# A TensorE multiply for every gathered row block in layer 3 of a graph network

## The chip, the core and the metric

The kernel runs on one NeuronCore of a Trainium2 chip. The metric is the time on the device in microseconds (us), the median of several executions. One execution is also profiled; its trace gives the start of each instruction on TensorE (PE, with its weight loads as PEld), VectorE (DVE), ScalarE (ACT), GpSimd (POOL) and SyncE (SP), the packets of the DMA engines, and the clock that TensorE was granted.

## What is computed

A graph of 3125 nodes (256 features each) and 50000 edges goes through four layers. Each layer is a graph step and a feed-forward step (mixture of experts or selected tokens), each added to the node features. The change touches the graph step of the last layer, which takes for every node the maximum over its neighbours' projected features:

```python
x = x + _L3_gnn_ref(_layernorm(x, axis=-1), edge_index, ...)

def _L3_gnn_ref(x, edge_index, W_proj, b_proj, W_l, b_l, W_r, gamma, beta):
    n = x.shape[0]
    loops = jnp.arange(n, dtype=edge_index.dtype)
    src = jnp.concatenate([edge_index[0], loops])
    dst = jnp.concatenate([edge_index[1], loops])
    xp = jax.nn.relu(x @ W_proj.T + b_proj)
    agg = jax.ops.segment_max(xp[src], dst, num_segments=n)
    out = agg @ W_l.T + b_l + x @ W_r.T
    out = jax.nn.relu(out)
    mean, var = jnp.mean(out, axis=0), jnp.var(out, axis=0)
    return (out - mean) * jax.lax.rsqrt(var + BN_EPS) * gamma + beta
```

## The kernel before

The nodes are ordered by their number of incoming edges and cut into NT = 25 tiles of 128, one node per partition. A tile's edges are processed in rounds: in one round every node of the tile takes one neighbour. RND lists the rounds of each tile (32 for the first, 9 for the last), OFF their running sum, and SR = 413 is their total. The few edges beyond these rounds go through a loop (`rounds_beyond`, `body3`) that runs only when there are any.

The program is one stream of instructions for each engine. The layers before this stage use a planner that orders the instructions by estimated costs. Layer 3's graph step doesn't use it: its loop stands in a `manual_schedule` block, so each engine gets its instructions in the order in which the code is written.

At the end of layer 2 the projected features relu(x W_proj + b) are written to the DRAM table `tab3`, and kept in ACC, where they are the node's own contribution to the maximum. XN holds the normalized features. Then the stage runs as follows.

- `look(r)` (L2376) takes a buffer of 128x256 from a pool of ROWS = 24 buffers and has GpSimd gather one row of `tab3` into each partition (an indirect DMA; the instruction is recorded under the helper's line L136). Round r's gather is issued right after round r - 24 has been used, and 24 are issued ahead of the loop.
- For each tile, TensorE transposes the tile's features XN (`turned`, L1651, two transposes into a PSUM bank of the tag `tp`), and ScalarE copies them to g_xt (L1653).
- For each round of the tile, VectorE takes the maximum of ACC and the gathered block (L2395), in place.
- At the seventh round of a tile, VectorE takes the batch statistics of the tile before it (`stats`, L2384), which read that tile's result Y (c_y in the profile).
- After the tile's last round, TensorE transposes the maxima (L1651), ScalarE copies them to g_at (L1653), and TensorE multiplies in two halves of 128 output features: two products with W_r on g_xt (L2405) and two with W_l on g_at (L2407), added up in one bank of the tag `mm`. ScalarE applies bias and relu and writes Y (L2408).

The PSUM banks of the stage are set by the call `psums(tp=3, mm=4)`: three for transposes, four for products. The matrices are float32. The identity used in transposes is `ident`. After the stage the statistics are combined (L2414) and the feed-forward step of layer 3 follows (from L2422), again under the planner, with expert products (L1982, L1986), gathers of expert results (ro_g) and the scatter of the output.

The shared helper `turned` and the gathering helper:

```python
    def gather(dst, table, idx):
        return nc.gpsimd.indirect_dma_start(
            out=dst, out_offset=None, in_=table, in_offset=bass.IndirectOffsetOnAxis(ap=idx, axis=0))
```

Of the kernel before, what the change touches and what calls it, by code (L numbers as in the profile page):

```python
# [13 lines left out]
OP = mybir.AluOpType  # L14
# [5 lines left out]
P = 128  # L20
# [75 lines left out]
def tile_gnn_ffn(ctx: ExitStack, tc: tile.TileContext, a: dict, out: bass.AP):  # L96
    nc = tc.nc
# [6 lines left out]
    @contextmanager  # L104
    def psums(**bufs):
        with tc.tile_pool(name="psum", bufs=1, space=PSUM) as p:
            before = dict(banks)
            banks["pool"], banks["bufs"] = p, bufs
            yield
            banks.update(before)  # L110

    def ps(tag, shape):
        return banks["pool"].tile(shape, F32, name=tag, tag=tag, bufs=banks["bufs"][tag])
# [35 lines left out]
    ident = per.tile([P, P], F32, name="ident")  # L149
# [96 lines left out]
    def load_w(pool, w, name):  # L246

        k, n = w.shape
        t = pool.tile([P, k // P, n], F32, name=name)
        nc.sync.dma_start(t, w.rearrange("(k p) n -> p k n", p=P))  # L250
        return t
# [207 lines left out]
    with tc.If(uns > 0):  # L459

        rec = dram.tile([E, RW], F32, name="rec")
        with tc.tile_pool(name="srt", bufs=1) as ep, tc.tile_pool(name="srt2", bufs=2) as eb, \
# [25 lines left out]
            for b in range(ET // BT):  # L488
                s = slice(b * BT, (b + 1) * BT)
                n = BT * EP  # L490
                row = eb.tile([P, n], I32, name="s_row")
# [24 lines left out]
                r = eb.tile([EP, BT, RW], F32, name="s_rec")  # L516
# [10 lines left out]
            for b in range(ET // BT):  # L527
                s = slice(b * BT, (b + 1) * BT)
                r = eb.tile([EP, BT, 8], F32, name="s_back")
# [932 lines left out]
    with tc.tile_pool(name="f1", bufs=1) as fp, tc.tile_pool(name="f1b", bufs=2) as fb, psums(mm=3, y=3, tp=2):  # L1462
# [60 lines left out]
        with tc.If(tie > 0):  # L1523

            with tc.tile_pool(name="f1t", bufs=1) as tp_:
                row = tp_.tile([P, NX], F32, name="f_row")
# [50 lines left out]
        for t in range(NT):  # L1577
            nc.tensor.matmul(pl.rearrange("p i k -> p (i k)"), fl[:, t, :], vals[:, t].rearrange("p i k -> p (i k)"),
                             start=(t == 0), stop=(t == NT - 1))
# [264 lines left out]
    class Experts:  # L1844
# [292 lines left out]
        def combine(self, t):  # L2137
# [7 lines left out]
                free.t = f  # L2145
            return f

    tab3 = dram.tile([NP, D], F32, name="tab3")

    with tc.tile_pool(name="g2", bufs=2) as gp, \  # L2150
# [60 lines left out]
        xin, rows = {t: At() for t in order2}, {t: [] for t in order2}  # L2211
# [139 lines left out]
    with tc.tile_pool(name="w3", bufs=1) as wp:  # L2351
# [3 lines left out]
        def halves(name, k):  # L2355
            t = wp.tile([P, 2], F32, name=name)
            nc.sync.dma_start(t, a[k].rearrange("(k p) -> p k", p=P))
            return t

        ga, be, bl = halves("c_ga", "L3_gnn_gamma"), halves("c_be", "L3_gnn_beta"), halves("c_bl", "L3_gnn_b_l")  # L2360
        with tc.tile_pool(name="g3", bufs=2) as gp, psums(tp=3, mm=4):
            wl = load_w(gp, a["L3_gnn_W_l"], "c_wl")
            wr = load_w(gp, a["L3_gnn_W_r"], "c_wr")


            def body3(rc, live):
                si = wp.tile([P, NT], I32, name="z_si")
                nc.vector.tensor_copy(si, rc[:, :, 0])
                for t in range(NT):
                    g = gp.tile([P, D], F32, name="g_row", bufs=24)  # L2370
                    gather(g, tab3, si[:, t : t + 1])
                    nc.vector.scalar_tensor_tensor(ACC[:, t, :], g, live[:, t : t + 1], ACC[:, t, :],
                                                   op0=OP.mult, op1=OP.max)
            rounds_beyond(wp, body3)

            def look(r):  # L2376
                if r < SR:
                    rows[r] = gp.tile([P, D], F32, name="g_row", bufs=ROWS)
                    gather(rows[r], tab3, srcI[:, r : r + 1])

            def stats(t):
                h = NV if t == NT - 1 else P
                for i in range(2):
                    nc.vector.bn_stats(bs[:, i, t, :], Y[:, i, t * P : t * P + h])  # L2384

            rows = {}
            with tc.manual_schedule(engines={EN.PE, EN.DVE, EN.Activation, EN.Pool, EN.SP}):
                for r in range(ROWS):
                    look(r)
                for t in range(NT):  # L2390
                    u = ACC[:, t, :]
                    xt = gp.tile([P, 2, P], F32, name="g_xt")
                    turned(xt, XN[:, t, :])
                    for r in range(OFF[t], OFF[t + 1]):
                        nc.vector.tensor_tensor(u, u, rows.pop(r), op=OP.max)  # L2395
                        look(r + ROWS)
                        if t and r == OFF[t] + 6:
                            stats(t - 1)
                    at = gp.tile([P, 2, P], F32, name="g_at")
                    turned(at, u)  # L2400
                    for i in range(2):
                        py = ps("mm", [P, P])
                        o = slice(i * P, (i + 1) * P)
                        for k in range(2):
                            nc.tensor.matmul(py, wr[:, k, o], xt[:, k, :], start=(k == 0), stop=False)  # L2405
                        for k in range(2):
                            nc.tensor.matmul(py, wl[:, k, o], at[:, k, :], start=False, stop=(k == 1))  # L2407
                        nc.scalar.activation(Y[:, i, t * P : (t + 1) * P], py, AF.Relu, bias=bl[:, i : i + 1])  # L2408
                stats(NT - 1)
# [5 lines left out]
        r = rsqrt(mv[:, :, 1], 2, wp)  # L2415
# [6 lines left out]
        with tc.tile_pool(name="f3", bufs=1) as fp, psums(tp=2, mm=2, y=2, u=2):  # L2422
            g3, b3 = halves("f_ga", "L3_ffn_gamma"), halves("f_be", "L3_ffn_beta")
# [117 lines left out]
```

## Time and profile before

| what | value |
|---|---|
| median of 3 runs | 4229.56 us (4227.59 to 4244.47) |
| the profiled execution | 4229.5 us |
| its span, first to last instruction | 4227.7 us |
| TensorE busy | 2697.7 us, 64% of the span |
| VectorE busy | 1946.6 us, 46% |
| GpSimd busy | 1758.5 us, 42% |
| ScalarE busy | 845.3 us, 20% |
| mean granted TensorE clock | 0.778 of full speed |
| layer 3's gathers, first to last start | 3179.3 to 3769.0 us |

A group line in the profile reads: line, engine, operation, written tile <- read tiles, shapes, count | busy us, mean ns of one | idle us of the engine just before these instructions, and what ended most of it. "issue" stands for no wait that the profile shows, "remote" for a semaphore update that the profile can't put down to an instruction or a DMA near it. In the page's digit rows the span is cut into 40 slices of 105.7 us; each digit is a busy share (or the clock) in tenths. A matmul's end in the records is modelled, its start is recorded. Windows lines give the bounds of a stretch, its length, then busy us and instruction count of PE, PEld, DVE, ACT and POOL, the granted clock, the share of the DMA engines and GB/s.

### The profile page before, as it was taken

What the parts mean: (1) busy time and instruction counts of PE and PEld (TensorE: products, weight loads), DVE (VectorE), ACT (ScalarE), POOL (GpSimd) and SP (SyncE); (2) the same over time, 40 slices, a digit from 0 to 9 for tenths busy, and PEclk for the clock granted to TensorE, in tenths of its full rate; (3) what the DMA queues carried; (4) which work ended last, traced back from release to release, by engine and by line L of the source; (5) the groups of instructions that cost most, each with busy time, mean ns of one, the idle gap of its engine ahead of it and who ended that gap; (6) DMA issues with size and microseconds to landing.
All of it is one profiled execution on the core that took longest, in us unless ns stands there. A gap on an engine that the chain in (4) does not pass through costs nothing. (4 is left out here: it accounts for less than half of the span.)

```text
span 4227.7 us, 46661 instructions
## 1 busy us (share of the span) xinstructions
PE 2697.7 (64%) x12940; PEld 2134.4 (50%) x12940; DVE 1946.6 (46%) x7501; ACT 845.3 (20%) x1803; POOL 1758.5 (42%) x1996
## 2 busy tenths in 40 slices
PE   1688999989889999948411365365670112137875
PEld 0566878767677878737310254254550111125653
DVE  3445666665665555442344333444662233245300
ACT  1112232221122222211100021122220000013322
POOL 4342333341253333002466544544437666643323
PEclk9878999999799999968755576577775555566987
DMA  7766455452243444113233254365523333323543
GB/s 223 223 190 187 129 157 144 130 154 65 76 118 107 118 133 126 52 48 107 73 93 91 86 175 141 107 185 168 174 90 101 87 92 88 92 81 107 158 159 100
DMA packets 275971, 521.46 MB, mean 123 GB/s; under 512 B 53609, under 2 KB 176897, under 8 KB 275685
## 3 DMA queue, kind: packets, MB, share of 16 engines
q0 software_dynamic: 105344, 306.57, 25.0%
q1 hardware_dynamic: 159598, 201.27, 15.6%
q10 hardware_dynamic: 10742, 10.34, 0.8%
q8 instruction: 114, 1.87, 0.2%
q14 instruction: 173, 1.41, 0.1%
HBM read 431.19 MB, written 86.78 MB: 123 GB/s over the span
## 5 line engine op out<-in xcount | busy, mean ns | idle before, releaser
L136 POOL DMA_INDIRECT g<-tab,m_si x521 | 498.0, 956 | 989.9 <-DVE mt L890 526.5
L136 POOL DMA_INDIRECT g_rows<-tab,srcI x413 | 401.9, 973 | 300.4 <-DVE ACC L2273 157.3
L136 POOL DMA_INDIRECT g_row<-tab,srcI x413 | 400.4, 970 | 196.3 <-issue 104.6
L880 PEld LDWEIGHTS c<-s,g 128*128 128x128 f32 x2084 | 345.8, 217 | 166.7 <-issue 83.9
L880 PE MATMUL c<-s,g 128*128 128x96 f32 x2084 | 356.1, 299 | 100.1 <-issue 38.2
L887 PE MATMUL pw<-w_d,f 65*128 65x256 f32 x1042 | 374.4, 445 | 14.2 <-DVE mt L890 11.9
L919 PE MATMUL f<-w_rel,aT 128*126 128x256 f32 x1600 | 372.6, 383 | 0.1
L884 ACT COPY aT<-c 128x384 f32<-128x384 f32 (+1 forms) x323 | 237.1, 737 | 595.7 <-PE c L880 397.5
L1982 PE MATMUL mm<-ro_xt,ro_w 128*128 128x192 f32 (+3 forms) x928 | 255.9, 428 | 122.3 <-ACT ro_h L2063 73.1
L919 PEld LDWEIGHTS f<-w_rel,aT 128*126 128x126 f32 x1600 | 300.2, 190 | 50.5 <-issue 5.3
L1651 PE MATMUL tp<-ident,ACC 128*128 128x128 f32 x50 | 16.1, 424 | 462.5 <-DVE ACC L2395 357.2
L890 DVE TENSOR_TENSOR mt<-pw,g 128x256 f32<-128x256 f32 x521 | 218.7, 420 | 159.0 <-PE pw L887 83.8
L1986 PE MATMUL y<-ro_w,ro_h 128*96 128x256 f32 (+2 forms) x1040 | 263.6, 409 | 33.5 <-ACT ro_h L2063 19.1
L1982 PEld LDWEIGHTS mm<-ro_xt,ro_w 128*128 128x128 f32 x928 | 183.8, 221 | 178.4 <-ACT ro_h L2063 80.5
L1651 PEld LDWEIGHTS tp<-ident,ACC 128*128 128x128 f32 x50 | 7.1, 199 | 470.5 <-issue 441.1
L1986 PEld LDWEIGHTS y<-ro_w,ro_h 128*96 128x96 f32 (+2 forms) x1040 | 190.4, 189 | 86.9 <-ACT ro_h L2063 23.1
L1037 PE MATMUL w<-w,b_h 128*126 128x256 f32 x800 | 218.5, 398 | 11.1 <-ACT xt L950 3.0
L1028 PE MATMUL w<-xt,w 128*128 128x252 f32 (+1 forms) x832 | 221.3, 392 | 6.3 <-issue 3.4
L140 POOL DMA_INDIRECT xg<-XX,ro_pos x100 | 101.6, 1016 | 287.6 <-issue 136.5
L2273 DVE SCALAR_TENSOR_TENSOR ACC<-g_rows,g_e,ACC 128x256 f32<-128x256 f32 x413 | 200.9, 486 | 43.9 <-DVE ACC L2273 19.9
L2395 DVE TENSOR_TENSOR ACC<-ACC,g_row 128x256 f32<-128x256 f32 x413 | 173.2, 424 | 67.1 <-DMA g_row<-tab,srcI 48.0
L2240 PE MATMUL pu<-w_s,a_xt 128*128 128x256 f32 x100 | 45.9, 606 | 231.5 <-DVE ACC L2268 104.8
(580 smaller groups left out, 4791.0 us busy)
## 6 DMA issues: line engine op xcount, KB each, us to landing
ro_w<-in_L_ffn_blocks SPq DMA_DIRECT2D x58, 514.0 KB
ro_w<-in_L_ffn_blocks SPq DMA_DIRECT2D x58, 512.0 KB
f<-in_attr_t SPq DMA_DIRECT2D x521, 32.5 KB
xg<-zero SPq DMA_DIRECT2D x78, 200.0 KB
b_at<-in_edge_attr SPq DMA_DIRECT2D x100, 125.0 KB
tabr<-v SPq DMA_DIRECT2D x12, 758.0 KB
g<-tab,m_si POOLq DMA_INDIRECT x521
g_rows<-in_L_ffn_blocks SPq DMA_DIRECT2D x14, 514.0 KB
```

The lines of the kernel that those rows point to most:

```text
L136: return nc.gpsimd.indirect_dma_start(out=dst, out_offset=None, in_=table, in_offset=bass.IndirectOffsetOnAxis(ap=idx, axis=0))
L880: nc.tensor.matmul(pc[:, h, o : o + GW], g[:, h * P : (h + 1) * P], sums[k][0], start=True, stop=True)
L884: nc.scalar.copy(aT[:, :, :, b : b + n * GN].rearrange("p k r n -> p k n r"), pc[:, :, : n * GW].rearrange("p k (n r) -> p k n r", r=16))
L887: nc.tensor.matmul(pw, feats.pop(k), wd, start=True, stop=True)
L890: nc.vector.tensor_tensor(mt[0], pw, rows.pop(k)[:, D:], op=OP.mult)
L919: nc.tensor.matmul(cur["f"][:TN], aT[:, h, r, :], wrel[:, h, r, :], start=(r == 0 and h == 0), stop=(r == 15 and h == 1))
L1028: nc.tensor.matmul(ph, w["01"][:, e, k, i * P : (i + 1) * P], xt[:, k, : n * TN], start=(k == 0), stop=(k == 1))
L1037: nc.tensor.matmul(py, last[:, k, i * TN : (i + 1) * TN], w["02"][:, e - 1, k, :], start=(k == 0), stop=(k == 1))
L1982: nc.tensor.matmul(ph, w[:, o : o + P], xt[:, k, :], start=(k == 0), stop=(k == 1))
L1986: nc.tensor.matmul(py, h[:, i, s], w[:, i * D : (i + 1) * D], start=(i == 0), stop=(i == self.fc - 1))
L2273: stt(u, g[:, r, :D], e[:, r0 + r : r0 + r + 1], u, op0=OP.mult, op1=OP.add)
L2395: nc.vector.tensor_tensor(u, u, rows.pop(r), op=OP.max)
```

## The change

Every round of layer 3 gets one more TensorE instruction: a product of the gathered block's first 128 columns with the identity, written to a PSUM bank of a new tag `idle` with one buffer. Nothing reads that bank. It stands before the maximum of the same round. The rest of the program is the same.

```diff
+    def busy(row):
+
+        nc.tensor.matmul(ps("idle", [P, P]), ident, row[:, :P], start=True, stop=True)
+
...
-        with tc.tile_pool(name="g3", bufs=2) as gp, psums(tp=3, mm=4):
+        with tc.tile_pool(name="g3", bufs=2) as gp, psums(tp=3, mm=4, idle=1):
...
                     for r in range(OFF[t], OFF[t + 1]):
-                        nc.vector.tensor_tensor(u, u, rows.pop(r), op=OP.max)
+                        g = rows.pop(r)
+                        busy(g)
+                        nc.vector.tensor_tensor(u, u, g, op=OP.max)
                         look(r + ROWS)
```

## The prediction

> **What bounds the kernel now.** I read the page first (engine shares, 40 slices, costliest groups). The chain of waits that ended last covers only the last 230 us, so for layer 3 I took the windows, waits and timeline of 3178 to 3782 us, where its gathers run. From the page:
>
> ```profile
> POOL 4342333341253333002466544544437666643323
> PEclk9878999999799999968755576577775555566987
> ...
> L136 POOL DMA_INDIRECT g_row<-tab,srcI x413 | 400.4, 970 | 196.3 <-issue 104.6
> ...
> L1651 PE MATMUL tp<-ident,ACC 128*128 128x128 f32 x50 | 16.1, 424 | 462.5 <-DVE ACC L2395 357.2
> ...
> L2395 DVE TENSOR_TENSOR ACC<-ACC,g_row 128x256 f32<-128x256 f32 x413 | 173.2, 424 | 67.1 <-DMA g_row<-tab,srcI 48.0
> ```
>
> In slices 31 to 36 GpSimd is the busiest engine, TensorE's clock is at half, and TensorE mostly waits for the maxima of L2395. The windows view of the stage, and of one long run of gathers in it (busy us, with counts, of PE, PEld, DVE, ACT, POOL; then clock, DMA share, GB/s):
>
> ```profile
> 3178.00:3782.00 604.00, 111.58 (x498) 99.39 (x498) 185.19 (x463) 35.23 (x99) 400.42 (x413) 0.54 0.31 90
> ...
> 3498.00:3563.00 65.00, 13.37 (x60) 11.86 (x60) 21.70 (x54) 3.23 (x9) 48.67 (x50) 0.55 0.35 100
> ```
>
> TensorE is busy 18% of the stage, VectorE 31%, GpSimd 66%. Gathers start 1.25 us apart when nothing stops them (0.95 busy and 0.30 between, below). The first starts at 3179.3 and the last at 3769.0: 589.7 us for 412 steps, 1.43 us each. So 589.7 - 412 x 1.25 = 75 us are lost; 65 of them lie in ten pauses of GpSimd (10.7, 6.6, 1.7, 8.3, 2.0, 7.3, 8.4, 7.9, 7.5 and 7.3 us in the timeline, less 0.3 each), the rest in gathers that take 1.0 to 1.1 us. The waits view says where the pauses come from:
>
> ```profile
> ACT c_y L2408 <- remote: 302.5, 24, 22.0
> DVE c_bs L2384 <- ACT c_y L2408: 173.0, 21, 25.5
> POOL g_row L136 <- DVE ACC L2395: 87.9, 86, 10.7
> ```
>
> GpSimd waits for a row buffer, VectorE for the statistics of the tile before, these for ScalarE's c_y, and that for something called remote. The timeline shows what (start, duration, idle before):
>
> ```profile
> 3401.63 0.42 PE L2407 MATMUL mm<-g_at,c_wl 128*128 128x128 f32 x1
> ...
> 3401.84 0.63 PE L1651 MATMUL tp<-ident,XX 128*128 128x128 f32 x2
> ...
> 3409.14 0.95 POOL L136 DMA_INDIRECT g_row<-tab,srcI  x1 [0.30 <-issue]
> 3410.39 0.95 POOL L136 DMA_INDIRECT g_row<-tab,srcI  x1 [0.30 <-issue]
> 3416.86 0.37 ACT L2408 ACTIVATE c_y<-mm,c_bl 128x128 f32<-128x128 f32 x1 [17.80 <-remote]
> 3417.26 0.29 DVE L2384 BATCH_NORM_STATS2 c_bs<-c_y 128x6 f32<-128x128 f32 x1 [22.06 <-ACT c_y L2408]
> 3418.32 0.37 ACT L2408 ACTIVATE c_y<-mm,c_bl 128x128 f32<-128x128 f32 x1 [1.09 <-remote]
> ```
>
> The last multiply of the tile ends by its record at 3402.05, but the c_y that needs it starts at 3418.32, when TensorE's semaphore update arrives: 16 us late. In the whole trace such late updates come almost only inside unbroken runs of gathers, from 5 us (dense TensorE work) or 14 us (layer 3) after the run's start, and nearly all catch up 1 to 7 us after it stops. The stage is thus gathers plus pauses that TensorE's late releases cause.
>
> **What the Trainium skill says.** "TensorE: Matmul & The Clock Gate", Part 1: an idle window of about 3.4 us puts TensorE at half clock, sustained work brings it back. The trace agrees: grants change in steps of 3.41 us, the stage's mean is 0.54. "Perfetto Trace Analysis", Tensor Engine Instruction: the reported end is an estimate, and the semaphore goes out only when PSUM has acknowledged the writes. The trace agrees, with the 16 us above between end and release.
>
> **The change part by part.** Nothing is removed. Added are 413 multiplies of 128x128. A multiply of this size is two weight loads and two matmul records (L2405: 200 records for 100 multiplies). In a row records are 0.213 us apart (four in 1.06 us); a lone pair takes 0.66 us (L1651, 3424.53). So 413 x 0.66 = 273 us of TensorE time. Per tile of 16.5 rows that is 10.9 us, plus the tile's own 4.5 (3424.53 to 3429.07): 15.4, against 16.5 x 1.25 = 20.6 us of gathers. Were releases on time, all of it would lie beside the gathers and cost nothing.
>
> Moved: TensorE's order. The new multiplies of a tile stand behind the transposes of x_t and ahead of the transposes of its maxima. They are in time for these, since the maxima need the same rows.
>
> Added waits, by the instruction order of the changed program: each multiply waits for its gather and, having one bank, for TensorE's own release of the multiply before it, so a late release stops the next one; queued behind are the tile's transposes and products, for which ScalarE, the statistics and so VectorE wait. And a gather now needs its buffer back from TensorE as well as from VectorE, 24 rows later. This is the term that counts. TensorE's records per row go from 40 / 16.5 = 2.4 to 6.4.
>
> The trace doesn't show such multiplies inside a gather run, so I bound what TensorE gets released there. In the run from 3498 its first 80 records (loads and matmuls) are released within 19 us; the next 40 take from 3517 to 3565, 0.83 per us. In the expert stage's run from 2843 to 2871, 141 records start: 83 before the first late release, then 58 in 24.5 us, 2.4 per us. I take 1.5 as between, and keep both ends. A cycle: GpSimd starts 24 rows ahead. TensorE's first 80 records are 12.5 rows, in about 10 us; GpSimd issues 8, its lead is 19.5. Then 1.5 / 6.4 = 0.23 rows per us come back while 0.8 go out; the lead is 24 after 8 us more. A pause of 7 us follows, as now, with 1.6 rows trickling. Together 25 us for 14.4 + 1.6 = 16 gathers: 1.56 us each instead of 1.43, 413 x 0.13 = 54 us more. With 0.83 per us the same sum gives 1.66 us (+94), with 2.4 it gives 1.445 (+6).
>
> Other edits: VectorE's maxima read the same rows and are unchanged; the extra bank takes none from the transposes' 3 and the products' 4. A warmer clock would shorten a tile's 4.5 us of TensorE work, which lies beside the next tile's gathers: nothing, except in the last tile (about 2 us).
>
> **The sum** stands against the profiled 4229.5 us (span 4227.7), equal to the median of 4229.56: 4229.5 + 54 = 4283 us, its own range 4235 to 4324.
>
> **The rivals.**
> - *Faster: steady work keeps releases on time.* For it: summed over the updates of TensorE's semaphore, each against the record's end before it, lateness is 56 to 175 us per 100 us of this stage and 0 to 36 in the dense first 2000 us. If the 413 multiplies prevent it, the pauses go: at most 65 us, 4164 us; I put it at 4180. Against: the dense expert stages have remote waits too (ro_h of L2063: 129.9 us in 26 waits), again inside gather runs.
> - *No change.* The multiplies are released in time and the pauses stay: 4229 us. For it: 15.4 of 20.6 us per tile. Against: it needs TensorE to release 6.4 records per 1.25 us inside a run, 5 per us, against 0.83 to 2.4 seen.
> - *Much slower: no recovery.* When GpSimd is blocked, each multiply released lets one gather out; if this trickle keeps releases slow, a row costs 6.4 / 1.5 = 4.3 us. At 2 us per row, as when a fifth of the rows go so, 413 x 0.57 = 235 us: 4465. It decides once the single gathers delay releases as a run does. Against: in the first 2000 us gathers with gaps stand beside dense TensorE work with few late releases; for: one pause (3289 to 3299) didn't bring the releases back.
> - The change does what it says: all 413 multiplies are in the changed program, none dropped.
>
> **How the numbers follow.** Chances: 0.52 for the forecast at 4283, 0.12 for much slower, 0.13 for no change, 0.23 for faster. The range, 4165 to 4465, reaches the faster bound and the 2 us row; beyond lies part of the much slower case. Under 0.5% (21 us: 4208 to 4251) is what can't be told from no change. Of the forecast's 0.52 some 0.05 falls within; so slower 0.59, same 0.18, faster 0.23.
>
> **What would show it.** In the changed profile: 826 more matmul records in the stage; gathers released by TensorE's new multiplies instead of by L2395; starts of gathers 1.5 to 1.6 us apart on average and the stage some 650 us long; the c_y waits still remote. Wrong: gathers 1.25 us apart throughout (releases recovered), or the stage unchanged at 604 us. That the clock in the stage rises above 0.54 would by itself prove nothing.

## The result and the profile after

The changed kernel takes 4253.78 us (median of 19 runs, 4232.47 to 4268.72), the kernel before 4236.27 us (19 runs, 4225.16 to 4255.09): a ratio of 1.0036, 95% interval 1.0023 to 1.005. It is slower, as forecast, but by 17 us and not by 54: less than the 0.5% (21 us) that the prediction called too little to be told from no change, though over 19 runs the interval leaves no change out. The profiled execution's span grew from 4227.7 to 4250.9 us, by 23.2 us, and the trace divides them:

| stretch (us) | before | after | difference |
|---|---|---|---|
| start to the first gather of layer 3 | 3179.3 | 3182.4 | +3.1 |
| first to last gather start | 589.7 | 600.5 | +10.8 |
| last gather to the first f_yn of the next step (the tail) | 17.5 | 25.5 | +8.0 |
| the rest | 441.1 | 442.5 | +1.3 |

The first and last rows are code that the change doesn't touch; the other two add up to 18.8 us, near the 17.5 between the medians. From the page of the changed kernel (slices, then groups):

```profile
PEclk9868999998899999968655587586865555666987
...
L136 POOL DMA_INDIRECT g_row<-tab,srcI x413 | 401.6, 973 | 205.8 <-issue 74.2
...
L2150 PE MATMUL idle<-g_row,ident 128*128 128x128 f32 x826 | 300.9, 464 | 207.9 <-remote 145.4
```

All 826 new matmul records are there (L2150, mean 464 ns). GpSimd's idle time before its gathers is 205.8 us instead of 196.3; there lies most of the stage's loss. The windows view of the stage (same columns as before the change):

```profile
3182.00:3784.00 602.00, 378.48 (x1227) 272.86 (x1227) 179.17 (x445) 30.53 (x88) 401.65 (x413) 0.57 0.32 90
```

TensorE went from 111.6 to 378.5 us busy, while GpSimd's gathers still take 401.7: the multiplies themselves lie beside the gathers. The waits view (total, times, longest) says what stops GpSimd now:

```profile
ACT c_y L2414 <- remote: 124.3, 21, 8.8
...
POOL g_row L136 <- remote: 55.3, 25, 4.0
POOL g_row L136 <- DVE ACC L2401: 44.2, 86, 5.8
...
POOL g_row L136 <- PE idle L2150: 21.7, 67, 1.2
```

Before, GpSimd's waits for a buffer ended with VectorE's maxima, the longest after 10.7 us. Now the larger part ends with TensorE's release, and no wait of that kind is longer than 4.0 us. (Those put down to "remote" belong here too: in each stop of that kind an update of TensorE's semaphore is recorded 0.26 us before the gather starts.) ScalarE's waits for late releases fell from 302.5 to 124.3 us. One cycle in the timeline (start, duration, idle before):

```profile
3516.36 1.06 PE L2413 MATMUL mm<-g_at,c_wl 128*128 128x128 f32 x4
...
3517.64 0.63 PE L2150 MATMUL idle<-g_row,ident 128*128 128x128 f32 x2
...
3520.79 0.95 POOL L136 DMA_INDIRECT g_row<-tab,srcI  x1 [0.30 <-issue]
3524.45 0.37 ACT L2414 ACTIVATE c_y<-mm,c_bl 128x128 f32<-128x128 f32 x1 [7.39 <-remote]
3524.55 0.50 PEld L2150 LDWEIGHTS idle<-g_row,ident 128*128 128x128 f32 x2 [6.57 <-remote]
...
3524.76 0.94 POOL L136 DMA_INDIRECT g_row<-tab,srcI  x1 [3.03 <-remote]
```

The tile's last product ends by its record at 3517.42, the next tile's first multiply at 3518.27; neither is released. GpSimd issues three more gathers and then finds the next buffer still held by TensorE. Its last gather ends at 3521.74; 2.7 us later the releases arrive together (c_y and the next multiply start), and the gathers go on at once. The stop of the kernel before that the prediction shows, after the gather at 3410.39, ended so:

```profile
3419.61 1.01 POOL L136 DMA_INDIRECT g_row<-tab,srcI  x1 [8.27 <-DVE ACC L2395]
```

There the last release came 7.0 us after the gathers had stopped (c_y at 3418.32), and the statistics and maxima took another 1.3 us. The new pauses are shorter and there are more of them: 26 of over 1 us, 2.8 us in the mean, against ten with a mean of 6.5. The two longest, of 5.3 and 5.5 us, still end by way of a late c_y and VectorE's maxima, as before the change.

### The profile page after: what moved, and what is told of

The parts are those of the page before. It is cut to its first block, busy times and chain, and to the rows that moved or that the text cites. A ratio compares the mean times of both kernels' runs of the same rounds, so it can differ in the third digit from the quotient of the medians.

```text
span 4250.9 us, 48698 instructions
## 1 busy us (share of the span) xinstructions
PE 2982.9 (70%) x13766; PEld 2326.0 (55%) x13766; DVE 1947.1 (46%) x7501; ACT 844.1 (20%) x1803; POOL 1758.9 (41%) x1996
## 5 line engine op out<-in xcount | busy, mean ns | idle before, releaser
L136 POOL DMA_INDIRECT g_row<-tab,srcI x413 | 401.6, 973 | 205.8 <-issue 74.2
L2150 PE MATMUL idle<-g_row,ident 128*128 128x128 f32 x826 | 300.9, 464 | 207.9 <-remote 145.4
L887 PE MATMUL pw<-w_d,f 65*128 65x256 f32 x1042 | 379.1, 450 | 18.6 <-DVE mt L890 17.2
L919 PE MATMUL f<-w_rel,aT 128*126 128x256 f32 x1600 | 378.5, 387 | 0.0
L2150 PEld LDWEIGHTS idle<-g_row,ident 128*128 128x128 f32 x826 | 191.6, 288 | 314.3 <-remote 153.2
L1986 PE MATMUL y<-ro_w,ro_h 128*96 128x256 f32 (+2 forms) x1040 | 261.3, 406 | 26.7 <-issue 20.6
L1037 PE MATMUL w<-w,b_h 128*126 128x256 f32 x800 | 218.0, 397 | 10.6 <-issue 3.0
L2244 PE MATMUL pu<-w_s,a_xt 128*128 128x256 f32 x100 | 45.4, 601 | 229.4 <-DVE ACC L2272 118.2
```

The source lines that it names most:

```text
L136: return nc.gpsimd.indirect_dma_start(out=dst, out_offset=None, in_=table, in_offset=bass.IndirectOffsetOnAxis(ap=idx, axis=0))
L887: nc.tensor.matmul(pw, feats.pop(k), wd, start=True, stop=True)
L919: nc.tensor.matmul(cur["f"][:TN], aT[:, h, r, :], wrel[:, h, r, :], start=(r == 0 and h == 0), stop=(r == 15 and h == 1))
L1037: nc.tensor.matmul(py, last[:, k, i * TN : (i + 1) * TN], w["02"][:, e - 1, k, :], start=(k == 0), stop=(k == 1))
L1986: nc.tensor.matmul(py, h[:, i, s], w[:, i * D : (i + 1) * D], start=(i == 0), stop=(i == self.fc - 1))
L2150: nc.tensor.matmul(ps("idle", [P, P]), ident, row[:, :P], start=True, stop=True)
```

## Experiments

The kernel before was run beside every experiment, and it has two times: about 4230 us in some sittings, that is, runs made together on one chip (4236.27 with the result above, 4221.8 beside e8 to e10, 4228.0 beside m2) and about 3757 us in others (3753.09 to 3761.62, beside all the rest), always the same within a sitting. In the faster sittings the traces of the layer-3 stage hold not one late release. What makes the difference was not found; the chip alone doesn't, since one chip gave both (late releases in e8 to e10, none in m1 and m3). I call them sittings with late releases and on-time sittings, and compare only within a sitting.

The traces of the changed kernel in the two kinds of sitting differ in two more ways. Of the 500 us between their spans (4250.9 and 3751.3) 350 lie ahead of layer 3's gathers and 85 within them, so late releases or what goes with them cost more outside this stage than in it. And the trace with late releases holds 29,919 records of semaphore updates, the on-time trace (e5 below) 57,793, with the same 48,698 records of instructions. The waits above rest on the starts of instructions; latenesses are read from those updates that were recorded. Whether lost records and late releases have one cause, and whether the recording has a part in it, no run here tells.

### On-time sittings: the change by itself

e5 is the changed kernel as it stands.

> The changed kernel itself, once more. The first four runs were made where the kernel before takes 3759.6 us and TensorE's releases in the layer-3 stage are on time. If this run meets the same (before about 3760): theory (the change costs only where releases come late in gather runs) expects gathers 1.25 us apart (515 to 518 us first to last), a tail of 17 to 22 us and 3755 to 3768 us in all, no change against before. Rival (the hold on the buffers and the row multiplies cost 11 + 8 us by themselves): 3779. If it meets late releases again (before about 4236): 4254 as at first.

Measured 3761.95 us beside 3760.0: ratio 1.0001 (0.9987 to 1.0014). The page's rows and the stage's window:

```profile
L136 POOL DMA_INDIRECT g_row<-tab,srcI x413 | 390.6, 946 | 131.5 <-PE idle L2150 69.1
...
L2150 PE MATMUL idle<-g_row,ident 128*128 128x128 f32 x826 | 264.8, 415 | 170.5 <-DMA g_row<-tab,srcI 162.9
```

```profile
2832.00:3349.00 517.00, 353.07 (x1300) 264.77 (x1300) 183.54 (x456) 34.19 (x96) 390.65 (x413) 0.64 0.37 105
```

The hold is at work here too: TensorE's multiply is the last release before more than half of the gathers (69.1 us of idle time, 0.3 each), but it comes in time. 413 gathers take 515.2 us first to last, 1.25 each, and the tail is 11.8 us. So neither the multiplies, nor the hold on the buffers, nor the multiplies after the last gather cost anything that can be measured, as long as releases are on time.

The first four runs had been meant to split the cost, and met the same kind of sitting. e1 and e6 are the kernel before with later statistics, e2 the changed kernel with them:

```diff
-                        if t and r == OFF[t] + 6:
-                            stats(t - 1)
+                        if t > 2 and r == OFF[t] + 6:
+                            stats(t - 3)
...
-                stats(NT - 1)
+                for t in range(NT - 3, NT):
+                    stats(t)
```

> The kernel before, with a tile's statistics taken three tiles later (some 60 us of slack for a late c_y). If the ten pauses come from TensorE's late releases by way of c_y and the statistics, as the prediction says: the 65 us of pauses go, first to last gather takes 520 to 530 us instead of 589.7, the kernel takes about 4170 us (4236 - 65), and lateness inside the now unbroken run grows past 16 us. If VectorE or the gathers themselves are slow (rival): first to last gather stays at 575 to 590 us and the kernel at 4225 to 4240.

> The changed kernel with the same later statistics. If the change's pauses are TensorE's direct hold on the row buffers: first to last gather stays near 600 us (590 to 610) and the kernel at about 4250 us, though c_y no longer holds VectorE. If its pauses still come by way of c_y, as the prediction had them: they go here too, gathers 520 to 535 us and the kernel about 4185 us.

> The kernel before with statistics three tiles later, a second time. Where releases are on time (before about 3760) 3760 again. Where they come late (before about 4236): if the pauses run by way of c_y and the statistics, gathers 520 to 530 us instead of 589.7 and 4170 us in all; if VectorE or the gathers are slow in themselves, 4225 to 4240.

e3 and e11 take the identity in place of the rows (`busy(ident)` for `busy(g)`), and e4 leaves the new multiplies of the last two tiles out (`if t < NT - 2`).

> The changed kernel, but each new multiply takes the identity in place of the gathered rows: the same records on TensorE, no wait for a gather and no hold on a row buffer. Theory (the hold on the buffers and the multiplies after the last gather are the cost): the tail from last gather to the next stage falls from 25.5 to 17 to 19 us, the pauses are again those by way of c_y (5 to 8 us each), gathers 585 to 600 us, kernel 4236 to 4246. Rival (the number of records released, as the prediction's rate sum has it): gathers 610 to 640 us, since 6.4 records a row at 1.5 per us hold c_y back even longer, kernel 4260 to 4290.

> The changed kernel without the new multiplies of the last two tiles. Theory (they run one after the other behind the last gather, ahead of the tiles' own products): the tail falls from 25.5 to 17 to 19 us, gathers stay at 598 to 603 us, kernel about 4246, 7 to 8 less than the change. Rival (the tail is a late release that catches up): it stays at 23 to 26 us, kernel 4254.

> The new multiplies on the identity instead of the rows, again: the same TensorE records, but no hold on a row buffer and no wait for a gather. For a chip where TensorE's releases come late (before about 4230): if the change's short pauses (some 3 us, one per tile) come from the direct hold of TensorE on the buffers, they go, and the pauses are those by way of c_y again, 6 to 10 us each; with 6.4 records a row to be released in a run they come at least as often as before, gathers 590 to 625 us; the tail is 12 to 18 us; kernel 4225 to 4262. If the number of records sets the time at 1.5 records per us, as the prediction's sum has it: gathers 630 to 660, kernel 4275 to 4300. Where releases are on time (before about 3760): no change against before, as in e3.

Ratios to the kernel before: e1 1.0004 (0.9991 to 1.0017), e2 1.0003 (0.999 to 1.0017), e6 1.0005 (0.9993 to 1.0017), e3 0.999 (0.9981 to 1.0), e4 1.0003 (0.9992 to 1.0014), e11 0.9996 (0.9983 to 1.0009). All gather in 515 to 516 us. They tell nothing apart except this: without late releases there is nothing to tell apart.

e7 and e12 are the kernel before with breaks in the gathers:

```diff
+            hold = wp.tile([P, 512], F32, name="c_hold")
...
                         look(r + ROWS)
+                        if r % 16 == 15:
+                            for _ in range(6):
+                                nc.gpsimd.memset(hold, 0.0)
```

> The kernel before with some 3 us of plain GpSimd work (six clears of a 128x512 tile that nobody reads, about 0.5 us each) after every 16th gather, 24 times. Where releases come late (before about 4236): if unbroken gather runs are what delays them and a break of 3 us lets them catch up, as in the changed kernel, the ten pauses of 7 us go and 24 of 3 us come, gathers 590 to 605 us, 4240 to 4255 us. If breaks don't help (rival), they add to the pauses: gathers 650 to 665 us, 4300 to 4315. Where releases are on time (before about 3760) there are no pauses to save: 516 + 24 x 3 = 588 us, 3830 us in all.

> The kernel before with a break of 3.3 us in the gathers after every 16th (plain GpSimd work, measured in e7), again. For a chip with late releases (before about 4230): if unbroken runs delay the releases and a short break lets them catch up, hardly a pause by way of c_y is left, and the gathers take 516 + 25 x 3.3 = 595 to 605 us, kernel 4235 to 4250. If breaks don't help: 590 + 83 = 665 to 675 us, kernel 4310. Where releases are on time: 3838, as in e7.

Both met on-time sittings and took 3838.32 and 3838.28 us, ratios of 1.021 (1.0177 to 1.0243) and 1.0206 (1.0175 to 1.0237): 24 breaks of 3.3 us are paid in full there.

### Late releases: a later c_y

In e8 to e10 ScalarE is kept busy ahead of each tile's c_y (seven copies of a tile `hold` of 128x2048 onto itself); e9 does it in the changed kernel, e10 in the kernel before with later statistics.

```diff
                     turned(at, u)
+                    for _ in range(7):
+                        nc.scalar.activation(hold, hold, AF.Copy)
```

> The kernel before with ScalarE kept busy for some 16 us (seven copies of a 128x2048 tile onto itself, 1.9 to 2.4 us each) between a tile's g_at and its c_y: every c_y comes some 13 to 16 us late by construction. Where TensorE's releases are on time (before about 3760): if a late c_y stops VectorE at the statistics and so the gathers, a tile can't take less than 16 + some 8 us (statistics 0.6, the tile's other maxima 9.5 x 0.43, transposes and products 2.6, c_y 0.7), against 20.6 us of gathers, so first to last gather grows from 515 to 560 to 600 us, and the wait on L2384 and the last tiles' chain bring the kernel to 3860 to 3920. If 24 buffers are enough to ride over 16 us (rival): gathers stay at 515 to 520 and only the end grows by 16 to 20 us, 3780. Where releases come late (before about 4236) both are late together: 4320 or more.

> The changed kernel with the same busy ScalarE. Only c_y is made late here, TensorE's own releases are not. If the new multiplies cost nothing by their number and order: the same as with the kernel before (within 10 us, gathers within 5 us). If queueing on TensorE behind late work adds to it (rival): 20 us or more above that.

> The kernel before with the busy ScalarE and the statistics three tiles later. Theory: three tiles of slack take up 16 us per tile, gathers stay at 515 to 520 us, and only the end is later (the last tiles' c_y come one after the other, 20 to 45 us): 3780 to 3810. Rival (VectorE is stopped by something other than the statistics): 3860 to 3920, as without the slack.

e8 took 4267.34 us beside 4221.8 (ratio 1.0096, 1.0067 to 1.0126). The seven copies took 1.91 us each, 13.4 us per tile, and yet first to last gather stayed at 587.8 us: ScalarE's work runs while c_y would have waited for TensorE anyway (its waits for late releases fell from 302.5 to 103.6 us). Only the tail grew, from 17.5 to 59.0 us. My number (4320 or more) had added two delays that overlap. e9 took 4301.47 (ratio 1.0188, 1.0147 to 1.0229), 34 us above e8, with gathers of 615.4: the "same within 10 us" failed, and the change costs more when c_y is also held up; I didn't follow that further. e10 took 4292.39 (1.0167, 1.0126 to 1.0208): gathers 585.5 us, tail 88.8. Three tiles of slack did not remove the pauses. They let the first run last 212 us, and the pause after it was 21.6 us. That stop, too, came by way of c_y and the statistics: c_y waited 18.5 us for its release, the statistics for c_y, the maxima for the statistics and the next gather for a maximum. The slack put the stop off and was then used up.

### Twelve forms in one program

Since sittings differ, I put the forms into one program: the stage runs twelve times in a row, each time as another form. (The maxima are taken over the same rows again, which changes nothing.)

```diff
+            def stage(mul=None, last=NT, banks=1, lag=1, gap=0, every=16, pair=1):
...
+                            if mul and t < last:
+                                busy(g if mul == "row" else ident)
+                            nc.vector.tensor_tensor(u, u, g, op=OP.max)
+                            look(r + ROWS)
+                            if gap and r % every == every - 1:
+                                for _ in range(gap):
+                                    nc.gpsimd.memset(hold, 0.0)
...
+            for q in VARIANTS:
...
+                        nc.vector.tensor_copy(src2, srcI)
+                        stage(**q)
```

m1 met an on-time sitting, m2 late releases; the program and the forms are the same. Each is one execution.

> Twelve forms of the layer-3 stage in a row in one program (same result; a copy of the gather indices after a form's last statistics holds the next form back), so that all meet one chip. First to last gather of each, where releases come late (before about 4230): 1 as before 585 to 595 us, ten pauses of 7. 2 as changed 597 to 605, 25 pauses of 3; its tail (last gather to end of the statistics) 6 to 9 us longer than form 1's. 3 multiplies on the identity, no hold on rows: if the short pauses are TensorE's direct hold, pauses of 6 to 10 come back, 590 to 625; by the prediction's 1.5 records per us 630 to 660. 4 two idle banks: 597 to 605 if the wait for the predecessor costs nothing, else 585 or less. 5 none in the last two tiles: gathers as 2, tail as 1. 6, 7 statistics three tiles later, without and with multiplies: 520 to 530 and 597 to 605 if only VectorE's wait for c_y makes the pauses of before; 575 to 590 if releases fall behind in any unbroken run until something stops it (e10 speaks for this). 8 breaks of 3.3 us per 16 gathers: 595 to 605 if breaks let releases catch up, else 660. 9 breaks of 1.1 us: 540 to 550 if that is enough, else 590 to 615. 10 two tiles' products in one (24 records per tile, not 40): 560 to 575 if records per run set the pauses, else 585 to 595. 11 both: 540 to 555. 12 as 1 within 8. Where releases are on time (before about 3760): 515 to 518, and 8, 9, 11 25 breaks more.

> The twelve forms in one program again, for a run in which TensorE's releases come late (kernel before about 4230); where they are on time (before about 3760) the first such run's numbers are met within 3 us each. Where late, first to last gather: 1 as before 585 to 595 us, ten pauses of 7 us. 2 as changed 597 to 605, some 25 pauses of 3; tail 6 to 9 us longer than form 1's. 3 multiplies on the identity, no hold on rows: pauses of 6 to 10 us come back, 590 to 625, if the short ones are TensorE's direct hold; 630 to 660 by the prediction's 1.5 records per us. 4 two idle banks: 597 to 605 if the wait for the predecessor costs nothing, 585 or less if it does. 5 none in the last two tiles: gathers as 2, tail as 1. 6 and 7 statistics three tiles later: 520 to 530 and 597 to 605 if only VectorE's wait for c_y makes the pauses; 575 to 590 if releases fall behind in any unbroken run until something stops it. 8 breaks of 3.3 us per 16 gathers: 595 to 605 if breaks let releases catch up, 660 if not. 9 breaks of 1.0 us: 540 to 550 if that is enough, 590 to 615 if not. 10 two tiles' products in one (24 records per tile, not 40): 560 to 575 if records per run set the pauses, 585 to 595 if not. 11 both: 540 to 555. 12 as 1 within 8 us.

Worked out from the starts in the two traces (us; the tail runs here to the end of the form's last statistics; pauses are gaps above 2.2 us between starts, less 1.25 each; lateness is that of TensorE's semaphore updates against the record's end before them):

| form | m1: gathers, tail | m2: gathers, tail | m2: pauses | largest lateness |
|---|---|---|---|---|
| 1 before | 515.4, 8.3 | 590.0, 14.0 | 10, sum 64.5 | 41.2 |
| 2 the change | 515.9, 11.0 | 605.6, 23.1 | 27, sum 78.8 | 10.3 |
| 3 identity for rows | 515.4, 10.6 | 725.9, 31.8 | 11, sum 200.4 | 19.3 |
| 4 change, two idle banks | 515.8, 8.2 | 602.5, 13.7 | 25, sum 68.5 | 17.2 |
| 5 change, none in last two tiles | 515.4, 8.2 | 600.7, 16.3 | 27, sum 70.9 | 15.9 |
| 6 before, later statistics | 515.1, 8.2 | 587.4, 23.9 | 7, sum 65.6 | 52.0 |
| 7 change, later statistics | 515.2, 13.9 | 613.6, 45.4 | 30, sum 96.4 | 11.8 |
| 8 before, breaks of 3.3 us | 596.1, 10.4 | 604.2, 10.4 | 26, sum 84.3 | 11.5 |
| 9 before, breaks of 1.0 us | 541.6, 8.4 | 589.8, 15.3 | 31, sum 66.0 | 41.1 |
| 10 before, two tiles' products in one | 515.3, 36.6 | 583.5, 70.6 | 5, sum 54.0 | 34.1 |
| 11 as 10, breaks of 1.0 us | 540.0, 14.3 | 582.6, 42.5 | 27, sum 57.3 | 37.5 |
| 12 before again | 515.4, 8.2 | 594.9, 14.1 | 10, sum 68.1 | 41.8 |

Forms 1, 12 and 2 repeat the two kernels (590 to 595 and 605.6 us against 589.7 and 600.5), so differences of 5 us between forms mean nothing. The sums of forms 8, 9 and 11 contain their breaks (80 us of form 8's sum, 25 of form 9's). The tails overlap: on VectorE the copy that starts the next form comes ahead of the last tile's statistics, so in m2 the next form's gathers start 3.5 to 24 us after the last one of the form. Form 12 has no successor, and its tail (14.1) is like form 1's (14.0); but the tails of forms 6, 7, 10 and 11 (24 to 71 us) run mostly under the next form's gathers, and what they would be alone is not shown. The windows view of m2, forms 1, 2, 3, 6 and 8:

```profile
3188.00:3779.00 591.00, 104.63 (x460) 93.54 (x460) 178.53 (x446) 32.21 (x90) 400.20 (x413) 0.54 0.32 91
3788.00:4394.00 606.00, 381.19 (x1245) 277.66 (x1246) 179.51 (x448) 32.34 (x92) 401.03 (x413) 0.58 0.31 89
4409.00:5135.00 726.00, 310.27 (x1239) 219.53 (x1238) 178.26 (x445) 32.73 (x92) 399.96 (x412) 0.63 0.26 75
...
6384.00:6973.00 589.00, 96.92 (x450) 84.84 (x451) 182.39 (x457) 31.87 (x89) 397.11 (x413) 0.55 0.32 92
...
7597.00:8202.00 605.00, 123.42 (x559) 110.66 (x557) 184.67 (x461) 36.95 (x105) 468.30 (x557) 0.56 0.31 89
```

All stages have the same gathers on GpSimd (400 us; form 8 has 68 us of clears on top); only the stage's length differs.

*Form 3* is the surprise: the same TensorE work without the hold, and without the wait for the gather, takes 725.9 us, above both expectations (590 to 625, and 630 to 660). Its timeline:

```profile
4839.76 0.50 PEld L2164 LDWEIGHTS idle<-ident 128*128 128x128 f32 x2 [5.10 <-remote]
...
4844.64 0.50 PEld L2164 LDWEIGHTS idle<-ident 128*128 128x128 f32 x2 [4.39 <-remote]
...
4846.46 0.95 POOL L150 DMA_INDIRECT g_row<-tab,c_src  x1 [0.30 <-issue]
...
4851.64 0.50 PEld L2164 LDWEIGHTS idle<-ident 128*128 128x128 f32 x2 [2.29 <-remote]
...
4852.49 0.50 PEld L2164 LDWEIGHTS idle<-ident 128*128 128x128 f32 x2 [0.35 <-PE idle L2164]
...
4862.72 0.29 DVE L2400 BATCH_NORM_STATS2 c_bs<-c_y 128x6 f32<-128x128 f32 x1 [37.38 <-ACT c_y L2442]
...
4865.14 1.01 POOL L150 DMA_INDIRECT g_row<-tab,c_src  x1 [17.73 <-DVE ACC L2425]
```

Inside the gather run that ends here a multiply is released 4.9 to 5.7 us after the one before (9.2 us at first), and the next waits for it (one bank). GpSimd goes on regardless until the row buffers are full because VectorE waits at the statistics. Its last gather ends at 4847.41; only then do the multiplies run, 0.85 us apart, the tile's products behind them, c_y, statistics and maxima. The pause is recovery plus that whole backlog: 17.4 us. In the changed kernel the hold stops GpSimd before such a backlog exists. That the hold is what makes the difference is read from these two timelines; form 3 takes away two dependencies at once, and no run under late releases puts breaks or a hold back into it.

*Form 8*: the kernel before with breaks every 16 gathers and no new multiplies behaves like the change: 604.2 us, 8 us above what its breaks cost in m1, so hardly a pause is left besides the breaks. *Form 9*: breaks of 1.0 us gain nothing (589.8): six pauses of 5 to 8 us stay, 40 us in sum where form 1 has 64.5, and the breaks cost the 25 us that this saves. *Form 6*, later statistics, has seven pauses in place of ten, and the sum is as before (65.6). Each of its six pauses of over 5 us still ended by way of c_y and the statistics; the first:

```profile
6617.58 0.37 ACT L2442 ACTIVATE c_y<-mm,c_bl 128x128 f32<-128x128 f32 x1 [18.59 <-remote]
6617.98 0.29 DVE L2400 BATCH_NORM_STATS2 c_bs<-c_y 128x6 f32<-128x128 f32 x1 [18.66 <-ACT c_y L2442]
...
6618.87 1.00 POOL L150 DMA_INDIRECT g_row<-tab,c_src  x1 [20.86 <-DVE ACC L2425]
```

Three tiles of slack don't help because a release can come later than that: up to 52 us in this form. *Form 4*: two idle banks (and three instead of four for the products) bring the tail back from 23.1 to 13.7 us, as no multiplies in the last two tiles do (16.3, form 5): the longer tail is the last tiles' multiplies, each waiting for the release of the one before it. The next form's first gather, which starts once VectorE has taken the form's last maximum, shows the same: it comes 9.3, 15.4, 10.2 and 12.3 us after the last gather of forms 1, 2, 4 and 5. *Forms 7, 10 and 11*: form 7 took 613.6 us, above both expectations, and form 11 582.6, far above its 540 to 555; form 10, 6.5 us below form 1, lies between both of its expectations. Of the forms whose tail can be compared none beats the kernel before (gathers and tail 604.0 us in form 1, 605.1 in form 9).

What remains of the pauses is that they grow with the run. For a pause, the trace gives the length of the gather run before it and the time from the run's end to the last of the releases that it waited for:

| kernel | run of gathers, us | recovery after it, us |
|---|---|---|
| changed kernel | 15.2, 17.7, 20.1, 24.0, 27.8 | 2.1, 2.4, 2.8, 3.4, 3.7 |
| kernel before | 27.9, 48.0, 54.8, 63.6, 109.1 | 5.3, 5.9, 6.0, 7.1, 9.4 |

In these pairs recovery is about an eighth of the run (0.09 to 0.14; 0.19 after 27.9 us), and in the changed kernel 21 of the 24 pauses that leave over 2.2 us between starts lie at 0.13 to 0.18. But the run's length is not all of it. In the changed kernel a run of 26.5 us was followed by 5.5 us and the first, of 54 us, by 3.0. In the kernel before, runs of 22.8 and 24.0 us took 6.1 and 7.0 us, each after a pause of less than 2 us; and in form 6 a run of 24.0 us took 6.5 after a pause of 20.6. What made these longer is open.

The number of TensorE's records can be set apart from the run's length with form 8. Its runs of about 20 us hold 2.4 records a row, and in 15 of its 24 breaks late releases come 2.9 to 3.2 us after the last gather. The changed kernel, with 6.4 records a row, took 2.5 to 3.0 us after runs of 19 to 20.3 us. So at this length recovery is about the same with and without the new multiplies. The sums are near each other too: 64.5, 65.6 and 78.8 us in forms 1, 6 and 2, 12 to 15% of 516 us of gathers.

m3 to m6 are twelve more forms: the identity with breaks, the identity with two banks, 40 or 12 buffers, a multiply for every second row, rarer breaks. All four met on-time sittings.

> Twelve more forms in one program. First to last gather where releases come late (kernel before about 4230): 1 as before 588 to 596 us. 2 as changed 600 to 607. 3 multiplies on the identity 715 to 735, 11 pauses of 13 to 27 us. 4 the same with breaks of 3.3 us per 16 gathers: theory (what makes the change cheap is that its hold on the buffers breaks the gathers every 16 rows, so that each stretch's records are released near in time): 600 to 620; rival (the number of records, or the missing hold itself, makes form 3 slow): 700 or more. 5 identity, two banks: 715 to 735 if the records' number sets it, 600 to 650 if each multiply's wait for its predecessor's release does. 6 changed, 40 buffers: a looser hold breaks later, fewer and longer pauses, 620 to 670; rival 600 to 607. 7 a multiply for every second row: 593 to 600. 8 as before with 12 buffers: earlier, shorter pauses by way of c_y, 580 to 600. 9 as before, breaks of 3.3 us per 32: 556 to 570 if that lets a stretch's 80 records catch up, 590 or more if not. 10 breaks of 2.2 us per 32: 543 to 560, or 585 to 600. 11 breaks of 2.2 us per 24: 552 to 565, or 585 to 600. 12 as 1 within 8 us. Where releases are on time (before about 3760): 515 to 518 for all but 4 (597), 9 (555), 10 (543) and 11 (552).

> The same twelve forms again, for a run with late releases. First to last gather where they come late (kernel before about 4230): 1 as before 588 to 596 us. 2 as changed 600 to 607. 3 multiplies on the identity 715 to 735, 11 pauses of 13 to 27 us. 4 the same with breaks of 3.3 us per 16 gathers: theory (what makes the change cheap is that its hold on the buffers breaks the gathers every 16 rows, so that each stretch's records are released near in time): 600 to 620; rival (the number of records, or the missing hold itself, makes form 3 slow): 700 or more. 5 identity, two banks: 715 to 735 if the records' number sets it, 600 to 650 if each multiply's wait for its predecessor's release does. 6 changed, 40 buffers: a looser hold breaks later, fewer and longer pauses, 620 to 670; rival 600 to 607. 7 a multiply for every second row: 593 to 600. 8 as before with 12 buffers: earlier, shorter pauses by way of c_y, 580 to 600. 9 as before, breaks of 3.3 us per 32: 556 to 570 if that lets a stretch's 80 records catch up, 590 or more if not. 10 breaks of 2.2 us per 32: 543 to 560, or 585 to 600. 11 breaks of 2.2 us per 24: 552 to 565, or 585 to 600. 12 as 1 within 8 us. Where releases are on time (before about 3760): the numbers of the first such run within 3 us.

> The same twelve forms, third try for late releases. First to last gather where they come late (kernel before about 4230): 1 as before 588 to 596 us. 2 as changed 600 to 607. 3 multiplies on the identity 715 to 735, 11 pauses of 13 to 27 us. 4 the same with breaks of 3.3 us per 16 gathers: theory (what makes the change cheap is that its hold on the buffers breaks the gathers every 16 rows, so that each stretch's records are released near in time): 600 to 620; rival (the number of records, or the missing hold itself, makes form 3 slow): 700 or more. 5 identity, two banks: 715 to 735 if the records' number sets it, 600 to 650 if each multiply's wait for its predecessor's release does. 6 changed, 40 buffers: a looser hold breaks later, fewer and longer pauses, 620 to 670; rival 600 to 607. 7 a multiply for every second row: 593 to 600. 8 as before with 12 buffers: earlier, shorter pauses by way of c_y, 580 to 600. 9 as before, breaks of 3.3 us per 32: 556 to 570 if that lets a stretch's 80 records catch up, 590 or more if not. 10 breaks of 2.2 us per 32: 543 to 560, or 585 to 600. 11 breaks of 2.2 us per 24: 552 to 565, or 585 to 600. 12 as 1 within 8 us. Where releases are on time (before about 3760): the numbers of the first such run within 3 us.

> The same twelve forms, last try for late releases. First to last gather where they come late (kernel before about 4230): 1 as before 588 to 596 us. 2 as changed 600 to 607. 3 multiplies on the identity 715 to 735, 11 pauses of 13 to 27 us. 4 the same with breaks of 3.3 us per 16 gathers: theory (what makes the change cheap is that its hold on the buffers breaks the gathers every 16 rows, so that each stretch's records are released near in time): 600 to 620; rival (the number of records, or the missing hold itself, makes form 3 slow): 700 or more. 5 identity, two banks: 715 to 735 if the records' number sets it, 600 to 650 if each multiply's wait for its predecessor's release does. 6 changed, 40 buffers: a looser hold breaks later, fewer and longer pauses, 620 to 670; rival 600 to 607. 7 a multiply for every second row: 593 to 600. 8 as before with 12 buffers: earlier, shorter pauses by way of c_y, 580 to 600. 9 as before, breaks of 3.3 us per 32: 556 to 570 if that lets a stretch's 80 records catch up, 590 or more if not. 10 breaks of 2.2 us per 32: 543 to 560, or 585 to 600. 11 breaks of 2.2 us per 24: 552 to 565, or 585 to 600. 12 as 1 within 8 us. Where releases are on time (before about 3760): the numbers of the first such run within 3 us.

In all four every form without breaks gathers in 515 to 516 us, and the others pay their breaks (598, 555 to 556, 541 and 550 us). Whether breaks would rescue form 3, and how a looser hold or rarer breaks act under late releases, stays open.

## Why the prediction was right in direction and wrong in size

- *What bounds the stage.* Right: gathers 1.25 us apart, plus pauses from late releases. Every on-time run shows the stage without them: 515 us, no late update. The chain by way of c_y and the statistics was right as well: three tiles of slack in it (form 6, and e10) put the stops off but didn't take them away, and they still ended through it.
- *"All of it would lie beside the gathers and cost nothing", were releases on time.* Shown by e5: ratio 1.0001.
- *The added hold on the buffers as "the term that counts".* Right as the place: the new stops end with TensorE's release. Wrong as the danger: without it, and without the wait for the gather, the same multiplies cost 136 us (form 3 against form 1), with both 16.
- *The cycle sum.* Here the prediction failed, in the term "A pause of 7 us follows, as now". It was taken at its size from the kernel before, where four of the six pauses of about 7 us follow runs of 48 to 64 us, and set behind a run of 18. The measured pauses are 2.1 to 3.7 us in the stage's regular part (from 3387 us on). Two things go with that. GpSimd waits for TensorE directly, where before the statistics and maxima took 1.3 us after the release. And after runs of about 20 us releases came within some 3 us of the last gather, with the new multiplies or without them (form 8). Why two runs of 23 and 24 us of the kernel before took 6 to 7 us stays open.
  The pause was not the only wrong term: with 2.8 us for 7 and the rest as it stood, the sum gives 20.8 us for 15 gathers, 1.38 us each, less than the 1.43 of the kernel before. The release budget was off as well: some 120 records of multiplies and products were released nearly on time in about 17 us, and then none until the gathers stopped, where I had 80 in 10 us and then a slow stretch of 8. And the 1.43 contains about 0.02 us of gathers that take over 0.95 us, which the 1.56 leaves out. One cycle from 3500.17 to 3524.76 holds 17 gathers: 1.45 us each, not 1.56. Over 412 steps the growth is 10.8 us instead of 54.
- *The end of the stage.* I held the last tiles' extra work for nothing and a warmer clock for a gain of 2 us; the tail grew by 8.0. Form 4 puts that on the one bank.
- *The rivals.* "Steady work keeps releases on time" isn't borne out: the largest lateness fell from 41.2 to 10.3 us (forms 1 and 2), but breaks without a new multiply bring it to 11.5 (form 8), and the pauses came all the same. "No recovery" came true nowhere in the change; form 3, at 1.76 us a row, comes nearest to it. "No change" is true of every on-time sitting.

The signs named beforehand: 826 records, gathers released by the new multiplies and c_y still waiting for remote updates were met; 1.5 to 1.6 us per gather and a stage of 650 us were not.

## What to carry to other kernels

A stall seen in a profile is not a constant: before it is put into a sum for a changed kernel, ask what it depends on, here in good part on the unbroken run before it. Slack in a chain only helps when it is longer than the delay can grow: three tiles of it moved the stops of form 6 and saved nothing. A dependency that stops the fast engine early can be cheaper than none (form 2 against form 3); by the timelines, because it keeps a backlog from forming that would have to be worked off one by one. And where two sittings differ by 11% for the same program, a change must be judged in both: this one costs 17 us in one and nothing in the other.

## What the runs showed of the hardware

- TensorE's semaphore updates can come late while GpSimd issues indirect gathers without a break: one in 4.9 to 5.7 us in a run of form 3, against 0.043 us apart once the gathers stop (in the changed kernel at 3524.4). The Trainium skill, "TensorE: Matmul & The Clock Gate", Part 3, The cost: per-tile semaphore tail, gives 26 ns for each increment when they queue up; the catch-up is of that order, the updates inside the run are a hundred times slower.
- The same program takes 4228 or 3757 us, depending on whether this happens; nothing in the kernel decides it, and the chip alone doesn't. In each pair of traces of one program here the one with late releases holds about half of the other's records of semaphore updates, or fewer (29,919 against 57,793 for the changed kernel, 48,951 against 139,558 for m2 and m1).
- Late or not, a gather costs GpSimd 0.95 us as a rule (median 0.946 in both kinds of sitting) and the next starts 0.30 us later; 3.3 us of other GpSimd work every 16 gathers let TensorE's releases catch up as a stop does (form 8); 1.0 us does so only in part (form 9: 40 us of longer pauses are left of 64.5).
